# A mixture-of-experts block: expert outputs added by accumulating transfers into three DRAM sums, in place of one DRAM row for each token and choice

## The chip, the core and the metric

The kernel runs on one core of one Trainium2 chip. The metric is the device time in microseconds (us) of one execution. Three runs of the kernel before took 300.21, 301.05 and 305.1 us; their median is 301.05 us.

## What is computed

The input is x, two sequences of 512 tokens with 256 channels, so 1024 tokens. A first part (a gated recurrence over time, with layer norms) changes x. A second part is a mixture of experts, and this is where the change lies. Cut to what matters:

```python
probs = jax.nn.softmax(x @ gate_w.T, axis=-1)             # 64 experts
topk_w, topk_idx = jax.lax.top_k(probs, 6)                 # 6 experts for each token
topk_w = topk_w / jnp.sum(topk_w, axis=-1, keepdims=True)
combine = jnp.sum(one_hot(topk_idx, 64) * topk_w[..., None], axis=1)
h = silu(einsum('th,eih->tei', x, experts_w1))             # 176 hidden channels
y = einsum('tei,ehi->teh', h, experts_w2)
routed_out = einsum('teh,te->th', y, combine)
out = routed_out + shared_out                              # shared_out: one dense expert
```

Every output row is x plus the layer norm of this sum. Each token's routed output is thus the sum of six rows that six different experts produce, each with a weight.

## The kernel before, in words

**Tiles.** The 1024 tokens are 8 tiles of 128 (`NTT`). The 64 experts are taken in 32 groups of two (`G`, `NG`). An expert has room for one block of 128 tokens in the fast path; what an expert gets beyond that is handled by one further block (`further`, run once in steps between the groups as a "float"), and by a loop whose count is read at run time (`tc.For_i`, L1007). The loop's body is not entered for these inputs.

**Stages, in order of time.**

1. *Mixing* (0 to about 115 us). Channels are mixed, and for each token tile `token_tile` (L473) computes the gate, picks six experts, and finds for each choice a slot in a DRAM array `xs_d`. VectorE (DVE), ScalarE (ACT) and TensorE (PE) instructions are interleaved by the class `Turns` (L314), a small planner that emits pieces of several streams by estimated costs: each piece says `yield spent(n)`, and the planner's clock moves on by that. A removed piece therefore also shifts the places of the pieces behind it.
2. *Scatter.* Each token tile issues six indirect transfers on GpSimd (POOL) (L576) that copy the tile's rows into `xs_d`. A row of `tok` has the 256 channels, then 64 weights (`C:DEST`), then 64 destination numbers (`DEST:`), 384 words in all. The destination numbers are made by one running sum (scan) over the 64 experts on DVE (L561): the number of the row of `y_d` into which this token's output of this expert goes. `xs_d` is filled beforehand with blank rows (L173, four transfers of 3072 KB on the SyncE queue), whose destination number lies beyond the end, so that unused rows are skipped later.
3. *Experts* (about 140 to 266 us). For each group of two experts, SP loads the rows (`load`, L879, four groups ahead, five buffers `xg`); `turn` (L882) transposes them on PE and copies each row's weight and destination into `cols` (12 buffers); `up` and `turn_h` compute the hidden layer; `down` (L928) multiplies by the second matrix; ACT scales the result by the weight into `y` (L940, six buffers, each for a pair of experts); and `collect` (L863) issues an indirect transfer on POOL that writes the 128 rows of `y` to their rows of `y_d`. `y_d` has 6144 rows of 256 words, one for each token and choice. All 65 of these transfers are declared independent of each other. The weights are loaded by SP into 19 buffers, 13 of the 32 groups in buffers used before.
4. *Tail* (about 266 us to the end). Each queue waits for all the collects and passes the loop's barrier. Then 16 loads of 384 KB (L1021), half issued by SP and half by ACT, bring in six rows for each token (`yk`). `total_up` (L1025) adds three of them to the other three on DVE, and PE adds those and the shared output (`y_sh`) in PSUM; `measure` and `put_out` do the layer norm, add x, and store.

**Order of the work.** PE, DVE, ACT and SP run their instructions in the order in which the code emits them. POOL is not among those engines (`ORDERED`), so a scheduler places its instructions; it keeps the order of dependent ones. A transfer on POOL also takes one of eight completion counters in turn.

Of the kernel before, what the change touches and what calls it, by code (L numbers as in the profile page):

```python
# [18 lines left out]
P = 128  # L19
# [17 lines left out]
G = 2  # L37
NG = E // G
DEST = C + E
ROW = DEST + E  # L40
WROW = 2 * I + C
# [11 lines left out]
def block_kernel(ctx: ExitStack, tc, x, w_act, w_rec, w_val, gate, wa, wb, wb_one, sh_gu, sh_dn, out):  # L53
# [112 lines left out]
    nc.gpsimd.memset(blank[:, :DEST], 0.0)  # L166
    nc.gpsimd.iota(blank[:, DEST:].bitcast(I32), pattern=[[0, E]], base=int(FAR), channel_multiplier=0)

# [13 lines left out]


    
    first_i = const.tile([P, NTT], I32, name="first_i")
    for i in range(NTT):
        nc.gpsimd.iota(
            first_i[:, i : i + 1],
            pattern=[[0, 1]],
            base=TOPK * i * P - 1,  # L190
            channel_multiplier=TOPK,
        )
    first_f = const.tile([P, NTT], F32, name="first_f")
    nc.gpsimd.tensor_copy(first_f, first_i)
    y_d = dram.tile([NT * TOPK, C], F32, name="y_d")
    y_sh = data.tile([P, NTT, C], F32, name="y_sh")
# [148 lines left out]
    def spent(n):  # L345
        return 0.16 + n / 960
# [93 lines left out]

    hsh = carve(len(SH_CHUNKS), NT)
    tok = carve(NTT, ROW)
    sel = data.tile([P, NTT, E], BF16, name="sel")
    lg = data.tile([P, NTT, E + 10], F32, name="lg")
    nc.gpsimd.memset(lg[:, :, E : E + 2], NEG)
    none_sel = const.tile([P, E], BF16, name="none_sel")
    nc.gpsimd.memset(none_sel, 0.0)
    rank = data.tile([P, NTT, E], F32, name="rank")
# [24 lines left out]
    def token_tile(t, pv):  # L473
# [79 lines left out]
        for j in range(t):  # L553
# [5 lines left out]
        yield spent(E / 2)  # L559

        nc.vector.tensor_tensor_scan(  # L561
            tok[:, t, DEST:].bitcast(I32), sel[:, t, :], none_sel, first_f[:, t : t + 1], ALU.add, ALU.add
        )
        yield spent(2 * E)

# [190 lines left out]
    def further(now, f):  # L756
# [66 lines left out]
        nc.vector.tensor_reduce(wt, two, AX.X, ALU.add)  # L823
        nc.vector.tensor_mul(two, xg[:, DEST:].bitcast(I32), one)
        to = stat.tile([P, 1], F32, tag="to", name="to")
        nc.vector.tensor_reduce(to, two, AX.X, ALU.add)
        to_i = stat.tile([P, 1], I32, tag="to_i", name="to_i")
        nc.vector.tensor_copy(to_i, to)
        yield
# [30 lines left out]

    puts = []

    def collect(y, rows):  # L863
        ins = nc.gpsimd.indirect_dma_start(  # L864
            out=y_d[:, :],
            out_offset=bass.IndirectOffsetOnAxis(ap=rows.bitcast(U32), axis=0),
            in_=y,
            in_offset=None,
            bounds_check=TOPK * NT - 1,
            oob_is_err=False,  # L870
        ).ins

        tc.declare_no_dep(ins, group="puts", reason="rows of y_d are disjoint")
        tc.add_to_no_dep_group("puts", ins)
        puts.append(ins)

# [5 lines left out]
    def turn(xg, g):  # L882

        px = ps.tile([P, G, KC, P], F32, tag="pr", name="px", bufs=1)
        for q in range(G):
            for k in range(KC):
                nc.tensor.transpose(px[:, q, k, :], xg[:, q, ts(k, P)], ident)  # L887
        cols = hpool.tile([P, 2, G], F32, tag="cols", name="cols", bufs=12)
        flat = xg.rearrange("p q r -> p (q r)")
        for u, o in enumerate((C + g * G, DEST + g * G)):  # L890
            nc.vector.tensor_copy(cols[:, u, :].bitcast(I32), flat[:, o : o + ROW + 2 : ROW + 1].bitcast(I32))
        xT = hpool.tile([P, G, KC, P], F32, tag="xT", name="xT")
        nc.vector.tensor_copy(xT, px)  # L893
        return xT, cols
# [109 lines left out]
    count = stat.tile([P, 1], I32, tag="count", name="count")  # L1004
    nc.scalar.copy(count, total)
    left = nc.values_load(count[0:1, 0:1], min_val=0, max_val=NOV)
# [7 lines left out]
    tpool = ctx.enter_context(tc.tile_pool(name="tpool", bufs=3))  # L1014
    y_v = y_d.rearrange("(i p k) c -> p i k c", k=TOPK, p=P)
    half = TOPK // 2
    yks, pos, mvs, rstds = {}, {}, {}, {}
    for i in range(NTT):
        yks[i] = tpool.tile([P, TOPK, C], F32, tag="yk", name="yk", bufs=NTT)
        for eng, o in ((nc.sync, 0), (nc.scalar, half)):  # L1020
            ins = eng.dma_start(yks[i][:, o : o + half, :], y_v[:, i, o : o + half]).ins  # L1021
            for w in puts:
                tc.add_manual_dep(ins, w.name, SYNC, reason="reads what every block wrote")

    def total_up(i):  # L1025

        yk = yks.pop(i)
        po = pos[i] = ps.tile([P, C], F32, tag="ps", name="po")
        nc.tensor.matmul(po, ident, y_sh[:, i, :], start=True, stop=False)
        pieces = [(0, half)] if i < NTT - 2 else [(k, k + 1) for k in range(half)]  # L1030
        for o, u in pieces:
            nc.vector.tensor_add(yk[:, o:u, :], yk[:, o:u, :], yk[:, half + o : half + u, :])  # L1032
        for k in range(half):
            nc.tensor.matmul(po, ident, yk[:, k, :], start=False, stop=(k == half - 1))  # L1034

# [71 lines left out]
```

## Time and profile before

| what | value |
|---|---|
| median of three runs | 301.05 us |
| the profiled execution's own time | 299.47 us |
| its span, first to last instruction | 297.8 us |
| mean granted TensorE clock | 0.901 |
| busy: PE, DVE, ACT, POOL | 235.5, 149.0, 119.6, 124.9 us |
| HBM read, written | 46.53 MB, 33.16 MB |

How it is read: a group's row gives line, engine, operation, output and inputs, the count, busy time, mean time of one in ns, then the engine's idle time just before, and what ended most of it. A row of a timeline gives start, duration, engine, line, operation and, in brackets, the idle time before. A row of a table of stages gives the stretch, its length, each engine's busy time with the number of instructions, the granted clock, the DMA engines' mean busy share, and GB/s. In a DMA queue's row stand packets, MB, and the share of 16 engines' time; q0 is POOL's queue, q1 SP's, q10 ACT's. In names, `SPq` and `ACTq` are the queues of instructions that issue transfers.

### The profile page before, as it was taken

The numbers are of one execution on the slowest core, as the hardware profiler recorded it, in microseconds if no ns is written. First come the engines' busy times: TensorE is split into PE (matmuls) and PEld (weight loads), VectorE is DVE, ScalarE is ACT, GpSimd is POOL, SyncE is SP. The second block draws the span as 40 slices with busy tenths as digits, with TensorE's granted clock in tenths as the row PEclk, the third lists the DMA queues.
The fourth block names the chain that finished last, engine by engine and source line by source line (L and its number), as shares of the span: only waits on it lengthen the run. The fifth ranks groups of instructions, "written<-read, shape, count | busy, mean of one in ns | idle before, by whom it ended". The sixth has DMA issues, their size and how long they took to land. (4 is left out here: it accounts for less than half of the span.)

```text
span 297.8 us, 4388 instructions
## 1 busy us (share of the span) xinstructions
PE 235.5 (79%) x1258; PEld 187.0 (63%) x1258; DVE 149.0 (50%) x628; ACT 119.6 (40%) x341; POOL 124.9 (42%) x159
## 2 busy tenths in 40 slices
PE   1989833964875778966889999999999999921992
PEld 0778613853664656855767788888887787710881
DVE  3469899766759504931335423333333333201594
ACT  2494665266129428202234443333333333410241
POOL 6000006722751763780064455555555555550041
PEclk9999975885599969996999999999999999985799
DMA  7999999999662443439999999999655531116982
GB/s 239 369 402 400 391 333 351 400 391 330 263 231 100 159 161 129 167 128 345 357 343 357 350 361 359 364 357 330 203 162 157 157 111 54 60 57 206 407 306 77
DMA packets 44025, 77.58 MB, mean 261 GB/s; under 512 B 4885, under 2 KB 29578, under 8 KB 44000
## 3 DMA queue, kind: packets, MB, share of 16 engines
q1 hardware_dynamic: 36480, 58.04, 56.9%
q0 software_dynamic: 6368, 16.11, 14.7%
q10 hardware_dynamic: 1152, 3.15, 2.9%
q8 instruction: 10, 0.16, 0.2%
q14 instruction: 15, 0.12, 0.1%
HBM read 46.53 MB, written 33.16 MB: 268 GB/s over the span
## 5 line engine op out<-in xcount | busy, mean ns | idle before, releaser
L864 POOL DMA_INDIRECT y_d<-y,cols x64 | 63.1, 986 | 66.9 <-ACT y L940 55.1
L576 POOL DMA_INDIRECT xs_d<-arena,slot_i x48 | 47.7, 993 | 78.5 <-DVE m L395 40.9
L924 DVE COPY hT<-pht 128x256 f32<-128x256 f32 x32 | 13.6, 424 | 69.3 <-PE pht L922 67.7
L940 ACT ACTIVATE y<-py,cols 128x256 f32<-128x256 f32 x64 | 26.8, 470 | 29.3 <-PE py L937 27.5
L911 ACT ACTIVATE h<-ph 128x256 f32<-128x256 f32 x32 | 12.3, 384 | 48.2 <-PE ph L906 39.9
L906 PE MATMUL ph<-w_sb,xT 128*128 128x176 f32 x176 | 30.0, 313 | 0.0
L906 PEld LDWEIGHTS ph<-w_sb,xT 128*128 128x128 f32 x176 | 26.4, 190 | 0.3 <-issue 0.3
L599 PE MATMUL pgu<-x2T,sh_gu_sb 128*128 128x256 f32 (+1 forms) x96 | 25.5, 424 | 0.0
L893 DVE COPY xT<-px 128x512 f32<-128x512 f32 x32 | 21.8, 683 | 4.2 <-PE px L887 4.2
L395 DVE TENSOR_TENSOR m<-z 128x32 f32<-128x32 f32 (+7 forms) x92 | 21.9, 280 | 2.4 <-remote 1.7
L933 PE MATMUL py<-w_sb,hT 128*128 128x256 f32 x88 | 22.7, 380 | 0.0
L599 PEld LDWEIGHTS pgu<-x2T,sh_gu_sb 128*128 128x128 f32 (+1 forms) x96 | 18.9, 201 | 4.0
L458 PE MATMUL pv<-w_val_sb,z 128*128 128x256 f32 x32 | 11.4, 520 | 11.6 <-DVE z L398 10.1
L887 PE MATMUL px<-ident,xg 128*128 128x128 f32 x128 | 19.3, 273 | 0.8 <-DVE xT L893 0.8
L264 PE MATMUL pz<-xnT,arena 128*128 128x256 f32 x64 | 17.3, 434 | 1.7 <-ACT xnT L253 0.9
L264 PEld LDWEIGHTS pz<-xnT,arena 128*128 128x128 f32 x64 | 13.8, 220 | 4.9 <-ACT xnT L253 1.4
L1034 PE MATMUL po<-yk,ident 128*128 128x256 f32 x48 | 13.6, 425 | 4.0 <-DVE yk L1032 4.0
L933 PEld LDWEIGHTS py<-w_sb,hT 128*128 128x128 f32 x88 | 15.8, 190 | 1.3 <-DVE hT L924 0.2
L458 PEld LDWEIGHTS pv<-w_val_sb,z 128*128 128x128 f32 x32 | 7.9, 260 | 13.7 <-issue 9.7
L283 PE MATMUL pr<-arena,xnT 128*128 128x256 f32 x64 | 15.8, 403 | 0.0
L887 PEld LDWEIGHTS px<-ident,xg 128*128 128x128 f32 x128 | 15.0, 141 | 1.1 <-DVE xT L893 1.0
L1032 DVE TENSOR_TENSOR yk<-yk 128x768 f32<-128x768 f32 (+1 forms) x12 | 7.9, 689 | 15.3 <-DMA yk<-y_d 15.2
(203 smaller groups left out, 431.3 us busy)
## 6 DMA issues: line engine op xcount, KB each, us to landing
w_sb<-in_wa SPq DMA_DIRECT2D x22, 608.0 KB
xs_d<-blank SPq DMA_DIRECT2D x4, 3072.0 KB
xg<-xs_d SPq DMA_DIRECT2D x32, 384.0 KB
arena<-in_wa SPq DMA_DIRECT2D x10, 608.0 KB
yk<-y_d ACTq DMA_DIRECT2D x8, 384.0 KB
yk<-y_d SPq DMA_DIRECT2D x8, 384.0 KB
w_sb<-in_wb SPq DMA_DIRECT2D x22, 112.0 KB
tok_d<-arena SPq DMA_DIRECT2D x2, 768.0 KB
```

The source lines that it names most:

```text
L264: nc.tensor.matmul(pz[:, ri, :], w_act_sb[:, kk, ts(ri, P)], xnT[:, kk % KC, b, o : o + H], start=(kk == 0), stop=(kk == 3),)
L283: nc.tensor.matmul(pr[:, j, :], xnT[:, kk % KC, b, o : o + P], w_rec_sb[:, kk, :], start=(kk == 0), stop=(kk == 3),)
L395: nc.vector.tensor_mul(h, dst, low[:, u : u + 1].to_broadcast(shape))
L458: nc.tensor.matmul(pv, zs[c][:, ri, 1 + j * P : 1 + (j + 1) * P], w_val_sb[:, ri, :], start=(ri == 0), stop=(ri == 1),)
L576: ins = nc.gpsimd.indirect_dma_start(out=xs_d[:, :], out_offset=bass.IndirectOffsetOnAxis(ap=slot_i[:, t, k : k + 1].bitcast(U32), axis=0) ...
L599: nc.tensor.matmul(pgu[:n, u, :], sh_gu_sb[:, k, off : off + n], x2T[:, k, ts(c, H)], start=(k == 0), stop=(k == KC - 1),)
L864: ins = nc.gpsimd.indirect_dma_start(out=y_d[:, :], out_offset=bass.IndirectOffsetOnAxis(ap=rows.bitcast(U32), axis=0), in_=y, in_offset=None,
L887: nc.tensor.transpose(px[:, q, k, :], xg[:, q, ts(k, P)], ident)
L893: nc.vector.tensor_copy(xT, px)
L906: nc.tensor.matmul(ph[:, q, :], xT[:, q, k, :], w1[:, ts(k, I)], start=(k == 0), stop=(k == KC - 1))
L933: nc.tensor.matmul(py, hT[:, q, :], w2as[q], start=True, stop=False)
L940: nc.scalar.activation(y[:, q, :], pys[q], AF.Copy, scale=wts[q])
```

## The change

Six parts:

1. A row of `tok` and `xs_d` shrinks from 384 to 321 words: the 64 destination numbers become one, the token's own number, written once by a POOL iota. The eight scans on DVE (L561) go, with their planner costs and helper tiles.
2. `y_d` goes. Three DRAM arrays of 1024 rows (`s0_d` to `s2_d`, 1 MB each) are set to zero by three transfers on SP's queue, after the first eleven groups' weights.
3. `collect` adds instead of writing: `compute_op=ALU.add`, into the three sums in turn. The independence that was declared between collects is gone, so a collect waits until the one three back, which wrote to the same sum, has landed.
4. The weight and destination of a row are copied as before by two small DVE copies; in the further block two DVE instructions go.
5. The tail loads three rows for each token, by 24 transfers of 128 KB instead of 16 of 384 KB; DVE adds one pair, PE takes in the other row.
6. The count for the loop is copied by DVE instead of ACT.

In the instruction lists of the two kernels the engines' orders are else alike, but for small swaps of neighbours in the mixing stage (the planner's clock), and for one thing on POOL: the last of the 64 collects, which stood ahead of the loop, stands behind it. The loads of the tail on both queues wait for that collect's counter.

```diff
-ROW = DEST + E
+ROW = DEST + 1
+
+NACC = 3
...
-    nc.gpsimd.iota(blank[:, DEST:].bitcast(I32), pattern=[[0, E]], base=int(FAR), channel_multiplier=0)
+    nc.gpsimd.iota(blank[:, DEST:].bitcast(I32), pattern=[[0, 1]], base=int(FAR), channel_multiplier=0)
...
-    y_d = dram.tile([NT * TOPK, C], F32, name="y_d")
+    sums_v = []
+    for a in range(NACC):
+        s_d = dram.tile([NT, C], F32, name=f"s{a}_d")
+        sums_v.append((s_d, s_d.rearrange("(i p) c -> p i c", p=P)))
+        nc.sync.dma_start(sums_v[a][1], blank[:, :C].unsqueeze(1).to_broadcast([P, NTT, C]))
...
     tok = carve(NTT, ROW)
+    nc.gpsimd.iota(tok[:, :, DEST:].bitcast(I32), pattern=[[P, NTT], [0, 1]], base=0, channel_multiplier=1)
...
-        nc.vector.tensor_tensor_scan(
-            tok[:, t, DEST:].bitcast(I32), sel[:, t, :], none_sel, first_f[:, t : t + 1], ALU.add, ALU.add
-        )
-        yield spent(2 * E)
...
-    puts = []
+    sum_turns = cycle(range(NACC))
     def collect(y, rows):
-        ins = nc.gpsimd.indirect_dma_start(
-            out=y_d[:, :],
+        nc.gpsimd.indirect_dma_start(
+            out=sums_v[next(sum_turns)][0][:, :],
             out_offset=bass.IndirectOffsetOnAxis(ap=rows.bitcast(U32), axis=0),
             in_=y,
             in_offset=None,
-            bounds_check=TOPK * NT - 1,
+            bounds_check=NT - 1,
             oob_is_err=False,
-        ).ins
-
-        tc.declare_no_dep(ins, group="puts", reason="rows of y_d are disjoint")
-        tc.add_to_no_dep_group("puts", ins)
-        puts.append(ins)
+            compute_op=ALU.add,
+        )
...
-    nc.scalar.copy(count, total)
+    nc.vector.tensor_copy(count, total)
...
-        yks[i] = tpool.tile([P, TOPK, C], F32, tag="yk", name="yk", bufs=NTT)
-        for eng, o in ((nc.sync, 0), (nc.scalar, half)):
-            ins = eng.dma_start(yks[i][:, o : o + half, :], y_v[:, i, o : o + half]).ins
-            for w in puts:
-                tc.add_manual_dep(ins, w.name, SYNC, reason="reads what every block wrote")
+        yks[i] = tpool.tile([P, NACC, C], F32, tag="yk", name="yk", bufs=NTT)
+    for i in range(0, NTT):
+        for a in range(NACC):
+            (nc.sync, nc.scalar)[(i * NACC + a) % 2].dma_start(yks[i][:, a, :], sums_v[a][1][:, i, :])
...
-        pieces = [(0, half)] if i < NTT - 2 else [(k, k + 1) for k in range(half)]
-        for o, u in pieces:
-            nc.vector.tensor_add(yk[:, o:u, :], yk[:, o:u, :], yk[:, half + o : half + u, :])
-        for k in range(half):
-            nc.tensor.matmul(po, ident, yk[:, k, :], start=False, stop=(k == half - 1))
+        nc.tensor.matmul(po, ident, yk[:, NACC - 1, :], start=False, stop=False)
+        nc.vector.tensor_add(yk[:, 0, :], yk[:, 0, :], yk[:, 1, :])
+        nc.tensor.matmul(po, ident, yk[:, 0, :], start=False, stop=True)
```

More of the change, by code (lines that the diff above doesn't have):

```diff
@@ L180, in block_kernel @@
         load_weights(g)
[L185 to L191, printed above, removed]
-        )
-    first_f = const.tile([P, NTT], F32, name="first_f")
-    nc.gpsimd.tensor_copy(first_f, first_i)
-    y_d = dram.tile([NT * TOPK, C], F32, name="y_d")
+    sums_v = []
[3 more added lines that the diff above has]
+        nc.sync.dma_start(sums_v[a][1], blank[:, :C].unsqueeze(1).to_broadcast([P, NTT, C]))
     y_sh = data.tile([P, NTT, C], F32, name="y_sh")
@@ L445, in block_kernel @@
     nc.gpsimd.memset(lg[:, :, E : E + 2], NEG)
-    none_sel = const.tile([P, E], BF16, name="none_sel")
-    nc.gpsimd.memset(none_sel, 0.0)
     rank = data.tile([P, NTT, E], F32, name="rank")
@@ L559, in token_tile @@
         yield spent(E / 2)
-        nc.vector.tensor_tensor_scan(
-            tok[:, t, DEST:].bitcast(I32), sel[:, t, :], none_sel, first_f[:, t : t + 1], ALU.add, ALU.add
-        )
-        yield spent(2 * E)
         nc.vector.reciprocal(tsum, tsum)
@@ L823, in further @@
         nc.vector.tensor_reduce(wt, two, AX.X, ALU.add)
-        nc.vector.tensor_mul(two, xg[:, DEST:].bitcast(I32), one)
-        to = stat.tile([P, 1], F32, tag="to", name="to")
-        nc.vector.tensor_reduce(to, two, AX.X, ALU.add)
         to_i = stat.tile([P, 1], I32, tag="to_i", name="to_i")
-        nc.vector.tensor_copy(to_i, to)
+        nc.vector.tensor_copy(to_i, xg[:, DEST:].bitcast(I32))
         yield
@@ L889, in turn @@
         flat = xg.rearrange("p q r -> p (q r)")
-        for u, o in enumerate((C + g * G, DEST + g * G)):
-            nc.vector.tensor_copy(cols[:, u, :].bitcast(I32), flat[:, o : o + ROW + 2 : ROW + 1].bitcast(I32))
+        o = C + g * G
+        nc.vector.tensor_copy(cols[:, 0, :], flat[:, o : o + ROW + 2 : ROW + 1])
+        nc.vector.tensor_copy(cols[:, 1, :].bitcast(I32), xg[:, :, DEST].bitcast(I32))
         xT = hpool.tile([P, G, KC, P], F32, tag="xT", name="xT")
@@ L1014, in block_kernel @@
     tpool = ctx.enter_context(tc.tile_pool(name="tpool", bufs=3))
-    y_v = y_d.rearrange("(i p k) c -> p i k c", k=TOPK, p=P)
-    half = TOPK // 2
     yks, pos, mvs, rstds = {}, {}, {}, {}
     for i in range(NTT):
-        yks[i] = tpool.tile([P, TOPK, C], F32, tag="yk", name="yk", bufs=NTT)
-        for eng, o in ((nc.sync, 0), (nc.scalar, half)):
-            ins = eng.dma_start(yks[i][:, o : o + half, :], y_v[:, i, o : o + half]).ins
-            for w in puts:
-                tc.add_manual_dep(ins, w.name, SYNC, reason="reads what every block wrote")
+        yks[i] = tpool.tile([P, NACC, C], F32, tag="yk", name="yk", bufs=NTT)
+    for i in range(0, NTT):
+        for a in range(NACC):
+            (nc.sync, nc.scalar)[(i * NACC + a) % 2].dma_start(yks[i][:, a, :], sums_v[a][1][:, i, :])
     def total_up(i):
```

## The prediction

> **What bounds the kernel now.** I read the table of stages first, over the stretches that the order of the work suggests.
>
> ```profile
> 115.00:140.00 25.00, 20.46 (x90) 16.65 (x89) 11.13 (x48) 7.72 (x17) 14.94 (x17) 0.86 0.58 207
> 148.00:209.00 61.00, 59.23 (x375) 47.21 (x373) 23.93 (x92) 25.33 (x74) 33.24 (x34) 1.00 1.03 352
> 209.00:266.00 57.00, 53.25 (x335) 41.64 (x333) 18.89 (x69) 20.91 (x62) 30.88 (x32) 1.00 0.39 121
> 270.00:287.00 17.00, 12.43 (x43) 9.64 (x44) 8.86 (x21) 3.94 (x8) 2.04 (x3) 0.71 0.96 363
> ```
>
> The columns after the length are PE, PE's weight loads, DVE, ACT, POOL, the clock, the DMA share, GB/s. The experts' stage is bound by PE (59.23 of 61, 53.25 of 57 us). POOL is about half busy, and the DMA engines are full up to about 209 us (1.03) and then not (0.39). The tail from 270 to 287 is bound by its loads (0.96). So in the experts' stage a collect costs nothing unless POOL falls behind; in the tail bytes are time.
>
> Then the collects: the rows of groups, and the timeline.
>
> ```profile
> L864 POOL DMA_INDIRECT y_d<-y,cols x64 | 63.1, 986 | 66.9 <-ACT y L940 55.1
> L576 POOL DMA_INDIRECT xs_d<-arena,slot_i x48 | 47.7, 993 | 78.5 <-DVE m L395 40.9
> L561 DVE TENSOR_TENSOR_SCAN arena<-sel,first_f,none_sel 128x64 int32<-128x64 bf16 x8 | 2.7, 339 | 0.1
> ```
>
> ```profile
> 151.16 1.04 POOL L811 DMA_INDIRECT xg_f<-tok_d,src  x1 [0.30 <-issue]
> ...
> 157.03 0.98 POOL L864 DMA_INDIRECT y_d<-y,cols  x1 [2.22 <-ACT y L940]
> 157.67 0.22 DVE L821 TENSOR_TENSOR two<-xg_f,one 128x64 f32<-128x64 f32 x1 [4.47 <-DMA xg_f<-tok_d,src]
> ...
> 185.48 0.98 POOL L864 DMA_INDIRECT y_d<-y,cols  x1 [1.33 <-ACT y L940]
> 186.77 0.98 POOL L864 DMA_INDIRECT y_d<-y,cols  x1 [0.30 <-issue]
> 189.09 0.98 POOL L864 DMA_INDIRECT y_d<-y,cols  x1 [1.33 <-ACT y L940]
> 190.37 0.98 POOL L864 DMA_INDIRECT y_d<-y,cols  x1 [0.30 <-issue]
> ```
>
> They come in pairs, one pair each 3.61 us. With three sums, a collect and the one three back are 4.89 us apart (185.48 to 190.37), then 5.92, then 4.89: on average 5.42. That is the time a collect will have to land before POOL waits for it.
>
> How long does one take? The DMA queues in short stretches show POOL's queue moving. Between 159.5 and 161.5 us nothing of a collect moves; between 161.5 and 162.5 one does (0.09 MB); on an idle machine, from 256.75 to 257.25, the one issued at 255.29.
>
> ```profile
> q0 software_dynamic: 1, 0.00, 0.0%
> q0 software_dynamic: 48, 0.09, 27.0%
> q0 software_dynamic: 47, 0.10, 56.5%
> ```
>
> Counted in order through the irregular part of the stage, the burst at 161.5 is that of 157.03. So data starts 4.5 us after issue while the DMA engines are full, and 1.5 us after when idle (up to 2.5 in 209 to 226, beside `xg` loads). A burst lasts 0.75 us full, 0.35 idle. After it comes about 0.5 us until a waiter sees it. A plain collect thus lands in about 5.8 us under load and 2.5 to 3.5 us later.
>
> **The change part by part.**
>
> *Scans and rows.* Eight scans of 0.339 us go: 2.7 us of DVE. DVE has 9.07 of 10 us busy in 40 to 50, under 8 of 10 after; in the last tiles the scan stands directly ahead of work that PE waits for. I take half, -1.4 us; from -2.7 to +1 (the planner swaps neighbours). In the further block two DVE instructions of 0.22 us go where DVE has just waited for a gather: -0.4. Scatters stay: 48 of 0.99 us (a gather of 608-word rows takes 1.01, so width doesn't set it), and they are not what starts the experts: SP's first `xg` rows are there at 137.0, PE's warm-up ends at 140.4. The blank fill moves 10.5 MB instead of 12.6: up to -5 us of DMA time, nothing if rows of 1284 bytes are slower; the zeros add 3.1 MB, 8 us at 400 GB/s, behind the eleventh group's weights and ahead of SP's first store of `tok`, which only the gather at 151 needs. The cover is the DMA share of 0.35 to 0.6 from 80 to 130 us; without it both would cost a few us. The two `cols` copies, the pool iotas: 0, the same count and size or done in the first 5 us.
>
> *POOL's time for an accumulating collect* isn't in the trace. A gather of 48 rows takes 0.894 us, of 128 rows 1.012: 1.5 ns a row, the rest fixed. A third descriptor beside two would add about 0.1 us; twice the whole is the upper end, 2.0. I take 1.0 to 1.1; a collect with its 0.30 gap then needs 1.4 of the 1.8 us that it has.
>
> *Its landing.* Lower end: only the data takes longer. The Trainium skill (Collectives: The Full Stack, "Why ReduceScatter is half of AllGather") says that an add in the transfer needs two source reads on the same ring and halves the throughput. By that rule, 5.8 + 0.75 = 6.6 us under load, 3.3 after. The trace's row of plain collects alone (5.8) would give almost no wait. Upper end: the old row is read as late as first data comes now, 4.5 more: 10.3, and 5 later. The nearest row for such a read through POOL's queue is the gather above, issued at 151.16 and used at 157.67: 6.5 us. A read of that kind, then a write of what a plain idle collect needs behind its issue (2.5 - 1.0 = 1.5), and 0.75 for doubled data: 8.8 us under load. Later, 3.0 + 1.5: 4.5 us. I take these. A rule of the skill speaks for the wait being real: DMA: Bandwidth & Descriptors, "Rules for kernel authors", wants an accumulate on the same bytes to wait for the earlier one's semaphore, and the instruction list has that wait.
>
> *What the wait makes.* With 8.8 us, three collects take 8.8, one takes 2.96 us with the wait's own overhead, against 1.8 that come. Behind a waiting collect on POOL stand only further collects (and the gather of the further block, which is ahead of the first one that waits). They hold `y` buffers: six pairs. When a pair's buffer is wanted and the collect eleven before hasn't landed, ACT waits, and PE behind it for PSUM. I carried this through collect by collect, from the ready times of the trace: issue at the latest of ready, 1.28 us behind the last issue, and landing of the third before; 8.8 us up to 209, then 4.5. By 209 about 20 of 35 are issued; PE is held for 8.5 us in all; after that a collect takes 1.53, POOL catches up, and the last collect is 10.8 us late. With 6.6 and 3.3 the largest lag is 10.7 us, PE is never held, and at the end nothing is left. With 8.8 and 5: 17. With 10.3 and 5: 22. I take +10.
>
> *The end.*
>
> ```profile
> 265.03 0.99 POOL L864 DMA_INDIRECT y_d<-y,cols  x1 [1.97 <-ACTq L1007]
> 266.32 0.98 POOL L864 DMA_INDIRECT y_d<-y,cols  x1 [0.30 <-POOLq L1007]
> 270.11 10.31 ACTq L1021 DMA_DIRECT2D yk<-y_d  x8
> ...
> 280.45 1.28 ACT L1042 ACT_TABLE_LOAD   x1 [16.74 <-DMA yk<-y_d]
> ```
>
> Now the last collect lands 2.5 us after 266.32, the barrier takes 1.25, and the loads start at 270.1, 5.1 us behind the last but one. After the change the last stands behind the barrier: landing 4.5 + barrier 1.25 + 0.3 + landing 4.5 + 0.2 = 10.75, so the loads start 5.65 us later (3.25 with 3.3 us). Then 3.1 MB instead of 6.3 are read: at 400 GB/s 7.9 us less. But the layer norms follow. ACT is held in issuing loads; its last goes out when the 16th of 24 has landed, 8.7 us after the start (now 10.3 for the 8th of 16); the first root comes 1.7 us earlier. From there a tile takes about 1.25 us of DVE (0.36 + 0.43 + 0.18 + 0.13 + 0.16 us) instead of 1.75: four tiles, -2.0; the last tile has one add and one closing matmul instead of three: -1.4. Together -5.1. The tail is +0.5 on balance. The count on DVE (0.19 us) frees ACT of work that nothing waits for, since POOL reads it last: 0.
>
> *Sum* against the profiled execution's own 299.47 us: -1.4 - 0.4 + 10 + 0.5 = +8.7, 308.2 us. Its own time lies 1.6 under the median of 301.05, so on the runs' scale 309.8; I take 309.
>
> **The rivals.**
>
> *The wait is covered by the buffers* (34 in 100). Landing of 6.6 to 8 us under load and at most 4.5 after: POOL lags by 11 to 15 us and recovers before the end. For it: six buffers, half-empty POOL, 57 us with a DMA share of 0.39. Against it: the gather's 6.5 us. The sum is -1.4 - 0.4 + 0 to 2 - 1.9 to +0.5: 297 to 302, about 299.
>
> *Faster: the halved tail loads decide* (12). From 270 to 287 loads bound; if an accumulate lands like a plain collect when idle (2.5 us), the start is 1.65 later, and if the layer norms keep up, the loads' whole 7.9 us count: -6.2 - 1.8 - some of the scans: 291 to 293. It decides if the landing in the tail is under 3 us and PE is never held. Against it: ACT's held root and the collect behind the barrier.
>
> *POOL becomes the bound* (5). If an accumulating collect takes over 1.5 us of POOL, 1.8 with its gap is all the room; at 2.0, 64 x 2.3 = 147 us against 118: 20 to 30 late, 322. Against it: the 1.5 ns a row.
>
> **How the numbers follow.** The chain of sums holding PE has 46 in 100, at 309 (own range 303 to 317); covered 34 (295 to 302, with 3 more where small things only add); faster 12; POOL 5. 2% of 301.05 is 6 us, about what a measurement of this kernel can tell from no change. Slower: 46 + 5, of which a little stays under 307 as a little of the rest goes over: 0.51. Same: 0.37. Faster: 0.12. The range leaves out the faster case and most of POOL's: 295 to 318.
>
> **What would show it.** Right: POOL's collects waiting for a transfer instead of ACT's `y`, 2.5 to 3 us apart up to about 210, then 1.5; ACT's `y` waiting for a collect and PE's share under 9 tenths near 190 to 215; the last collect issued after the barrier. Landing: the distance of a waiting collect to the one three back. Wrong: collects still in pairs 3.61 us apart with `y` as the releaser (covered); POOL instructions of 1.5 us or more (POOL's case); first loads of the tail under 3 us later than the last but one's 5.1; and the scans, if the experts' stage doesn't start about 1.4 us earlier.

## The result and the profile after

The changed kernel takes 322.56 us, the median of four runs (321.95 to 327.63), against 303.08 us for the kernel before (300.21 to 306.78, four runs). The ratio is 1.070, with a 95% interval of 1.063 to 1.077; it compares undisturbed executions only, so it is not the quotient of these medians. The profiled execution has a span of 320.8 us, 23.0 more than before, at a mean granted clock of 0.868 (before 0.901). The experts' stage itself ran at nearly the same clock: 0.97 and 1.00 in its two stretches below, 1.00 and 1.00 before.

The two timelines give where these 23.0 us lie (rounded):

| stretch | before, us | after, us | difference |
|---|---|---|---|
| start to first collect | 148.5 | 151.5 | +3.0 |
| first collect to PE's last product for `y` | 113.6 | 115.7 | +2.1 |
| from there to the last collect but one ("POOL's tail") | 3.0 | 19.4 | +16.4 |
| from there to the start of the first load of the tail | 5.1 | 9.4 | +4.3 |
| from there to the end | 27.7 | 24.8 | -2.9 |

The rows behind the first three lines, before and after: the first collect, and PE's last product for `y`.

```profile
148.50 1.04 POOL L864 DMA_INDIRECT y_d<-y,cols  x1 [13.80 <-ACT y L940]
262.06 0.70 PE L937 MATMUL py<-arena,hT 48*128 48x256 f32 x4
...
151.50 1.66 POOL L850 DMA_INDIRECT s_d<-y,cols  x1 [13.85 <-ACT y L924]
267.22 0.70 PE L921 MATMUL py<-arena,hT 48*128 48x256 f32 x4
```

So most of the loss, 16.4 of 23.0 us, is one thing: PE is done 5 us later than before, and POOL is still issuing collects 19 us after that. The table of stages says the same; the two stretches of the experts' stage are moved by 3 us against those of the prediction, that of the tail by 26:

```profile
115.00:140.00 25.00, 20.20 (x107) 16.41 (x107) 12.31 (x58) 10.23 (x28) 15.08 (x17) 0.91 0.41 142
151.00:212.00 61.00, 58.18 (x361) 46.55 (x360) 22.12 (x85) 24.64 (x72) 38.59 (x25) 0.97 1.06 317
212.00:269.00 57.00, 55.41 (x349) 43.66 (x347) 20.40 (x75) 20.84 (x62) 46.27 (x30) 1.00 0.64 104
296.00:313.00 17.00, 11.79 (x40) 9.14 (x41) 7.54 (x28) 4.91 (x10) 2.38 (x4) 0.75 0.65 201
```

PE keeps its share (58.18 of 61, 55.41 of 57). POOL, the fifth engine column, gets through 25 instructions in the experts' first stretch where it had 34, and in their second it is busy for 46.27 of 57 us with 30 of them (30.88 with 32 before). In the tail the DMA engines are no longer full (0.65, 201 GB/s; before 0.96 and 363): half the bytes, read more slowly.

The groups of the two indirect transfers:

```profile
L850 POOL DMA_INDIRECT s_d<-y,cols x64 | 99.8, 1560 | 52.7 <-ACT y L924 21.1 <-issue 11.7 <-DMA s_d<-y,cols 9.7
L565 POOL DMA_INDIRECT xs_d<-arena,slot_i x48 | 48.1, 1003 | 81.7 <-DMA w_sb<-in_wb 45.4 <-ACT rank L563 14.8 <-issue 12.2
```

A collect that adds takes 1.56 us of POOL instead of 0.986. With the usual gap of 0.30, one collect can follow the other each 1.86 us; this is called POOL's period below. PE supplies one each 1.80 us (a pair in 3.61). The scatters are as short as they were, but the first now waits for a transfer on SP's queue.

The timeline of POOL, first under load, then later:

```profile
187.53 1.55 POOL L850 DMA_INDIRECT s_d<-y,cols  x1 [1.01 <-ACT y L924]
189.60 1.56 POOL L850 DMA_INDIRECT s_d<-y,cols  x1 [0.52 <-issue]
192.15 1.55 POOL L850 DMA_INDIRECT s_d<-y,cols  x1 [0.99 <-DMA s_d<-y,cols]
194.84 1.56 POOL L850 DMA_INDIRECT s_d<-y,cols  x1 [1.14 <-DVE cols L875]
197.37 1.55 POOL L850 DMA_INDIRECT s_d<-y,cols  x1 [0.97 <-DMA s_d<-y,cols]
199.57 1.56 POOL L850 DMA_INDIRECT s_d<-y,cols  x1 [0.65 <-DVE xT L877]
202.25 1.55 POOL L850 DMA_INDIRECT s_d<-y,cols  x1 [1.12 <-ACT y L924]
...
215.96 1.55 POOL L850 DMA_INDIRECT s_d<-y,cols  x1 [0.30 <-ACT y L924]
217.82 1.56 POOL L850 DMA_INDIRECT s_d<-y,cols  x1 [0.30 <-ACT h L895]
```

A collect and the one three back are 7.3 and 7.4 us apart (187.53, 194.84, 202.25): this is the landing under load, and a collect then takes 2.45 us. The idle time ahead of them is put down to various engines (`y`, `cols`, `xT`), which is an example of a wait for several semaphores: those had long been done, and the steady distance of three shows that it is the transfer. From 214 on the waits are nearly all gone, and then POOL's own 1.86 us sets the pace. Twenty collects after the first, POOL is 50.8 us behind it, where it was 38.3 before: 12.5 us late. At the last but one it is 18.6 later. The lag of the loaded stretch is never made up, and grows.

POOL's queue, over the stretches that follow the issue of the last collect at 292.25 (294.0 to 294.5, to 295.0, to 295.6; nothing moves from 292.1 to 294.0):

```profile
q0 software_dynamic: 14, 0.01, 57.6%
q0 software_dynamic: 49, 0.05, 75.8%
q0 software_dynamic: 80, 0.04, 52.1%
```

The burst takes about 1.4 us on an idle machine, where a plain collect's took 0.35. Over the whole execution:

```profile
q0 software_dynamic: 11824, 14.57, 23.0%
```

The queue has 11824 packets (6368 before) for fewer bytes, and 73.8 us of all 16 engines (23.0% of 320.8) instead of 43.8.

Last, the end:

```profile
286.61 1.56 POOL L850 DMA_INDIRECT s_d<-y,cols  x1 [0.38 <-issue]
292.25 1.55 POOL L850 DMA_INDIRECT s_d<-y,cols  x1 [4.08 <-issue]
295.99 1.30 SPq L1004 DMA_DIRECT2D yk<-s_d  x3
...
305.88 1.28 ACT L1021 ACT_TABLE_LOAD   x1 [34.34 <-DMA yk<-s_d]
```

The last collect stands behind the loop's barrier, 5.64 us after the one ahead of it. The loads start 3.74 us after that. ACT is held in issuing its loads for 9.9 us.

### The profile page after: what moved, and what is told of

It is laid out like the page before. It is cut to its first block, busy times and chain, and to the rows that moved or that the text cites. A ratio compares the mean times of both kernels' runs of the same rounds, so it can differ in the third digit from the quotient of the medians.

```text
span 320.8 us, 4343 instructions
## 1 busy us (share of the span) xinstructions
PE 233.6 (73%) x1242; PEld 185.1 (58%) x1242; DVE 143.1 (45%) x615; ACT 120.3 (37%) x340; POOL 161.5 (50%) x150
## 3 DMA queue, kind: packets, MB, share of 16 engines
q0 software_dynamic: 11824, 14.57, 23.0%
q10 hardware_dynamic: 1728, 1.57, 1.6%
## 5 line engine op out<-in xcount | busy, mean ns | idle before, releaser
L850 POOL DMA_INDIRECT s_d<-y,cols x64 | 99.8, 1560 | 52.7 <-ACT y L924 21.1
L890 PE MATMUL ph<-w_sb,xT 128*128 128x176 f32 x176 | 31.1, 322 | 0.0
L890 PEld LDWEIGHTS ph<-w_sb,xT 128*128 128x128 f32 x176 | 27.5, 197 | 0.3 <-issue 0.3
L588 PE MATMUL pgu<-x2T,sh_gu_sb 128*128 128x256 f32 (+1 forms) x96 | 26.4, 434 | 0.0
L1010 PE MATMUL po<-y_sh,ident 128*128 128x256 f32 x16 | 6.2, 476 | 24.0 <-issue 24.0
L917 PE MATMUL py<-w_sb,hT 128*128 128x256 f32 x88 | 22.6, 379 | 0.0
L1012 DVE TENSOR_TENSOR yk<-yk 128x256 f32<-128x256 f32 x8 | 3.3, 416 | 34.4 <-DMA yk<-s_d 34.4
L1010 PEld LDWEIGHTS po<-y_sh,ident 128*128 128x128 f32 x16 | 3.7, 242 | 25.0 <-issue 24.4
L258 PE MATMUL pz<-xnT,arena 128*128 128x256 f32 x64 | 16.0, 409 | 1.7 <-ACT xnT L247 1.0
L512 PE MATMUL pl<-gate_sb,x2T 128*128 128x64 f32 x32 | 7.7, 393 | 11.4 <-issue 8.0
L258 PEld LDWEIGHTS pz<-xnT,arena 128*128 128x128 f32 x64 | 12.9, 206 | 4.5 <-ACT xnT L247 1.4
```

What stands on the lines that cost most here:

```text
L258: nc.tensor.matmul(pz[:, ri, :], w_act_sb[:, kk, ts(ri, P)], xnT[:, kk % KC, b, o : o + H], start=(kk == 0), stop=(kk == 3),)
L588: nc.tensor.matmul(pgu[:n, u, :], sh_gu_sb[:, k, off : off + n], x2T[:, k, ts(c, H)], start=(k == 0), stop=(k == KC - 1),)
L850: nc.gpsimd.indirect_dma_start(out=sums_v[next(sum_turns)][0][:, :], out_offset=bass.IndirectOffsetOnAxis(ap=rows.bitcast(U32), axis=0), i ...
L890: nc.tensor.matmul(ph[:, q, :], xT[:, q, k, :], w1[:, ts(k, I)], start=(k == 0), stop=(k == KC - 1))
L917: nc.tensor.matmul(py, hT[:, q, :], w2as[q], start=True, stop=False)
```

## The experiments

**Theory A:** the loss takes two things together. The wait for the sum three back makes POOL lag while the DMA engines are full; and since an adding collect takes 1.86 us of POOL against a supply of 1.80, POOL never makes the lag up. Rivals: the wait alone (as predicted); POOL's time alone; the time that the adds take on the DMA engines, at PE's expense.

The runs fall into four groups, in each of which the kernel before was run again. It took 286.37 us (median) beside plain writes, eight and four sums, and adding before; 302.50 beside 384-word rows and both runs on the count; 300.54 beside two plain sums, bf16 rows and both runs with two copies; 300.45 beside the run with one copy. The first and the last group ran on the same chip at different times, so the 14 us between them aren't a property of the chip; what they are stays open. Across groups only ratios to the kernel before of the same group are compared, and stretches inside the experts' stage, where the granted clock was 0.97 to 1.00 in every profile.

**Plain writes: the wait, without adds.**

```diff
-            compute_op=ALU.add,
```

> The changed kernel with its collects writing instead of adding, so that the six outputs of a token overwrite each other in three arrays: the addition is left out, the waits on the collect three back stay. Theory A (it takes both: a wait under load that makes POOL late, and 1.86 us of POOL for each adding collect, which leaves no room to make it up): POOL's collect falls from 1.56 to 0.98 us, plain landing is 5.8 us under load, POOL lags by up to 5 us and has recovered by 266; the last collect ahead of the loop starts near 268 instead of 286.6, and the time is about 302 us. Rival B (the wait alone): the same if only the landing matters, since 5.8 us of landing in three turns are near the pace of 1.8. Rival C (something else in the new kernel, such as the row width, keeps the experts late): over 310.

Measured: 283.53 us, ratio 0.983 (0.977 to 0.989). The timeline of POOL:

```profile
182.86 0.98 POOL L850 DMA_INDIRECT s_d<-y,cols  x1 [2.88 <-DMA s_d<-y,cols]
184.24 0.98 POOL L850 DMA_INDIRECT s_d<-y,cols  x1 [0.40 <-DVE cols L874]
185.53 0.99 POOL L850 DMA_INDIRECT s_d<-y,cols  x1 [0.30 <-ACT h L894]
189.20 0.98 POOL L850 DMA_INDIRECT s_d<-y,cols  x1 [2.69 <-ACT h L894]
...
217.23 0.99 POOL L850 DMA_INDIRECT s_d<-y,cols  x1 [0.30 <-DMA s_d<-y,cols]
218.52 0.99 POOL L850 DMA_INDIRECT s_d<-y,cols  x1 [0.30 <-DMA s_d<-y,cols]
```

The wait is there (6.3 to 6.9 us from one collect to the third behind it), and POOL falls behind: twenty collects after the first it is 6.4 us late against the profile of the kernel before. But from about 205 on POOL runs at 1.29 us and has caught up by the end (115.8 us from the first to the last but one; 116.5 before). So the wait by itself costs nothing here, and the rest of the change seems to gain a little: 1.7% by the ratio, 1.0% by the medians of all executions, both under the 2% that would count as faster.

**Eight sums in turn: adds, nearly without the wait.** Three of the eight are set to zero and read back.

```diff
+NSUM = 8
...
-    for a in range(NACC):
+    for a in range(NSUM):
...
-    sum_turns = cycle(range(NACC))
+    sum_turns = cycle(range(NSUM))
```

> The changed kernel with eight sums in turn instead of three, so that a collect waits for the one eight back; only three are set to zero and only three are added in the tail, so five sums are left out of the output. Theory A: no wait is left; POOL's 1.86 us for each collect alone make the last ones about 4 us late instead of 18.6; about 308 us. Rival B (the wait alone): the collects come in pairs again and are not late; 304. Rival C (POOL's time alone makes the 18.6): no change, 322.

Measured: 292.96 us, ratio 1.022 (1.016 to 1.027). A collect takes the same 1.56 us, but the tail of POOL behind PE is gone: the last collect but one comes 4.4 us after PE's last product, where it is 19.4 with three sums. That takes the wait out of the change, and most of the loss with it. It is not all gone: from the first collect to the last but one are 123.8 us (115.8 with plain writes), 8.0 more where 3.9 was expected, and the rest lies in PE.

```profile
180.00:195.00 15.00, 13.24 (x81) 9.78 (x79) 4.82 (x16) 4.62 (x14) 12.56 (x9) 1.00 1.05 289
195.00:210.00 15.00, 13.65 (x88) 11.00 (x87) 5.83 (x20) 5.07 (x15) 10.83 (x8) 1.00 0.90 199
```

PE, the first engine column, is not full there (13.24 and 13.65 of 15), while the DMA engines have a share of 1.05 and move only 289 GB/s (the kernel before 363 between 180 and 195). In the changed kernel PE has 15.00 of 15 in both stretches.

**Four sums.** `NACC` is 4, and the tail adds two rows to the other two.

> The changed kernel with four sums, all added in the tail (two pairs on DVE, two rows on PE). Theory A: a landing of 7.4 us in four turns is 1.85, as much as POOL's own 1.86, so the wait adds almost nothing; the last collects are 4 to 6 us late; 1 MB more is read in the tail, +2.6 us; about 311 us. Rival B: 309. Rival C: 325.

Measured: 300.59 us, ratio 1.045 (1.036 to 1.053). It lies between three and eight sums, as it should if the wait grows shorter, but above the 311 us that were expected (some 1.03): four turns don't take the wait away. In the execution that was profiled, the longest of the four (303.17 us), POOL's tail is 8.3 us, also between the two.

**The kernel before with adding collects: adds, no wait at all.** `y_d` is set to zero beforehand.

```diff
     y_d = dram.tile([NT * TOPK, C], F32, name="y_d")
+    y_z = y_d.rearrange("(a i p) c -> a p i c", a=TOPK, p=P)
+    for a in range(TOPK):
+        nc.sync.dma_start(y_z[a], blank[:, :C].unsqueeze(1).to_broadcast([P, NTT, C]))
...
             oob_is_err=False,
+            compute_op=ALU.add,
```

> The kernel before with one change: its collects add into the 6144 rows of y_d, which six transfers set to zero behind the first weights. Every row is written once, so no collect waits for another. Theory A: POOL's collect takes 1.56 us, one each 1.86 against 1.805 that come: about 4 us late at the end, landing 1 us longer; +5 us, 306 to 308 us. Rival B (the wait alone): +1 us. Rival C (POOL's time alone makes the 18.6): +18 us, 320.

Measured: 300.12 us, ratio 1.045 (1.039 to 1.051), some 13 us where 5 were expected. POOL's tail is 4.4 us again, so POOL's time without the wait leaves POOL close behind PE. What was not expected is that PE itself is late: 121.8 us from the first collect to its last product. PE's waits between 180 and 210 us are led by the rows that SP loads:

```profile
PE px L891 <- DMA xg<-xs_d: 3.2, 4, 1.2
```

With adds at full pace these loads come late: the DMA engines have a share of 1.05 and move 295 GB/s between 180 and 195 us, where they moved 363 before. In the changed kernel this rival is not what costs the time, since PE is full there (15.00 of 15). (This kernel also writes 6.3 MB of zeros that the kernel before doesn't, before the first collect.)

**Rows of 384 words in the changed kernel.**

```diff
-ROW = DEST + 1
+ROW = DEST + E
```

The slices that fill and read the last words follow.

> The changed kernel with rows of 384 words again, of which the last 63 are not used. Theory: rows of 1284 bytes cost the blank fill as much time a row as those of 1536 or more, so the first scatter and the experts start late; with 384 words the first scatter starts near 46.5 instead of 50.1 and the first collect near 148.5 instead of 151.5; -3 us, about 319.5. Rival (the planner's new order or the clock of PE makes the experts late): first collect stays at 151.5, no change.

Measured: 324.85 us, ratio 1.075 (1.069 to 1.082), so no gain. But the profile shows what the narrow rows do. The stretch from 20 to 32 us, first with 321 words, then with 384:

```profile
20.00:32.00 12.00, 10.53 (x51) 8.97 (x50) 10.54 (x50) 6.90 (x11) 0.00 (x0) 1.00 1.07 306
```

```profile
20.00:32.00 12.00, 10.53 (x51) 8.97 (x50) 11.16 (x52) 6.89 (x12) 0.00 (x0) 1.00 1.06 399
```

The fill runs at 306 GB/s with rows of 1284 bytes, at 399 with 1536. A narrower row is not a quicker one: 2870 packets in these 12 us, against 3128. With 384 words the first scatter goes out at 46.54 us (46.22 before, 50.06 after), and the first collect at 147.07 (148.5 before, 151.5 after). Yet the last collect but one is at 286.56, as it was at 286.61: POOL eats the earlier start (139.5 us instead of 135.1 from the first collect to the last but one). No run shows why; with the experts 4 us earlier, more of the collects fall in the time in which the DMA engines are full, which fits theory A but is only argued.

**The count on ACT in the changed kernel, and on DVE in the kernel before.** Two kernels, the same line exchanged:

```diff
-    nc.vector.tensor_copy(count, total)
+    nc.scalar.copy(count, total)
```

> The changed kernel with the count copied by ACT again, which by the instruction list puts the last collect ahead of the loop. Theory: the last collect then follows the one before by 1.86 us and one landing and the barrier follow, so the loads of the tail start about 2.6 us earlier; about 320 us. Rival (the place of the last collect costs nothing, since its landing is hidden in the barrier): no change, 322.5.

> The kernel before with only the count copied by DVE instead of ACT, which by the instruction list puts the last collect behind the loop. Theory: two landings of 2.5 us and the barrier between them instead of one: the tail's loads start 6.75 us behind the last collect ahead of the loop instead of 5.1 behind the last but one, +1.7 us, a ratio of 1.005. Rival: no change, or a gain because the engines read the count earlier.

Measured: with the count on ACT 324.35 us, ratio 1.071 (1.065 to 1.078); the kernel before with the count on DVE 304.21 us, ratio 1.009 (1.006 to 1.011), a small loss that is clear of its interval. The end of the latter:

```profile
266.57 0.99 POOL L864 DMA_INDIRECT y_d<-y,cols  x1 [1.97 <-issue]
270.68 0.98 POOL L864 DMA_INDIRECT y_d<-y,cols  x1 [3.11 <-issue]
```

The one-instruction change of part 6 puts the last collect behind the loop: the two are 4.11 us apart instead of 1.29. It isn't the count alone that decides, though: in the changed kernel with two plain sums, and with plain writes and idle copies (both below), the count is on DVE too, and the last two collects are only 1.3 to 1.6 us apart, much as in the kernel before. Why the scheduler places the last collect in one way or the other isn't shown. In the changed kernel the count on ACT brings the loads' start from 9.4 to 6.4 us behind the last collect but one. The whole didn't become faster: in that execution the first collect came 3.1 us later than in the profiled one of the changed kernel, so this run alone leaves the price of part 6 in the changed kernel unsettled.

**Two plain sums in turn: a longer wait, without adds.**

```diff
-    sum_turns = cycle(range(NACC))
+    sum_turns = cycle(range(2))
...
-            compute_op=ALU.add,
```

> The kernel after, but with plain writes, and into two of the three sums in turn; the addition is left out and the third sum stays zero. A collect thus takes POOL's 0.98 us, and waits for the one two back. The wait by itself, made as long per collect as the prediction had it (there 8.8 us over three; here the 6.7 us between waiting collects of the run with plain writes, over two, 3.35 us). Theory (the wait holds PE if it is long enough; the recurrence of the prediction is right): under load collects 3.3 us apart, largest lag about 26 us, ACT's y waits for collects and PE is held by about 11 us, the last collect 11 to 16 us later than with three plain sums; ratio to the kernel before 1.02 to 1.04. Rival (only adds cost, by the time they take on POOL or on the DMA engines): as three plain sums, 0.98 to 0.99.

Measured: 324.25 us, ratio 1.078 (1.063 to 1.094), slower than expected. The timeline of POOL, and ACT's group for `y`:

```profile
173.63 0.98 POOL L850 DMA_INDIRECT s_d<-y,cols  x1 [4.51 <-DMA s_d<-y,cols]
174.92 0.99 POOL L850 DMA_INDIRECT s_d<-y,cols  x1 [0.30 <-issue]
180.48 0.98 POOL L850 DMA_INDIRECT s_d<-y,cols  x1 [4.57 <-DMA s_d<-y,cols]
181.77 0.99 POOL L850 DMA_INDIRECT s_d<-y,cols  x1 [0.30 <-issue]
```

```profile
L923 ACT ACTIVATE y<-py,cols 128x256 f32<-128x256 f32 x64 | 26.9, 471 | 60.0 <-DMA s_d<-y,cols 34.9 <-PE py L920 16.0 <-PE ph L889 5.6
```

A pair each 6.85 us, `y` waits 34.9 us for collects, and PE's part of the stage is 119.9 us (112.8 with three plain sums). So the wait is able to do alone what the prediction had it do, if it is long enough. The last collect but one is 22.6 us late instead of 11 to 16. The term that the expectation had too small is the landing after the load: there a collect takes 1.56 us on average, over a wait of two, so some 3.1 us, and more where both waits follow each other.

**Idle work on POOL: POOL's time without adds.** Behind each collect of the plain kernel, two small copies, and in a later run only the first:

```diff
+        for n in (C, 1):
+            nc.gpsimd.tensor_copy(junk[:, :n], y[:, :n])
```

> The kernel after with plain writes (the addition is left out), three sums in turn and the wait for the one three back kept, and with each collect two idle copies on POOL (128x256 and 128x1) that bring POOL's time for a collect to about the 1.86 us of an adding one. No adds on the DMA engines. Theory A (POOL's time and the wait together make the lag): with 6.7 us between waiting collects under load and 2.5 later, the last collect is 11 to 14 us later than with plain writes alone; ratio 1.02 to 1.03. Rival B (it is what the adds take of the DMA engines): as plain writes alone, 0.98 to 0.99.

> The kernel before with the same two idle copies on POOL behind each collect: POOL's time alone, no wait, no adds, no other bytes. Theory A: POOL is 3 to 4 us late at the end, ratio 1.01 to 1.015; the 1.045 of the kernel before with adding collects then holds some 9 us that are the transfers' own. If POOL's time were all of it: 1.045.

> As the plain writes into three sums with two idle copies, but with one copy (128x256, 0.41 us) behind each collect: POOL's period should fall between the 1.29 us of plain collects and the 2.03 of two copies, I expect 1.57 to 1.8. The addition is left out. Theory A (a lag built up by the wait under load, about 10 us here with 6.7 us between waiting collects, is made up only as far as POOL's period is below the supply of 1.80): last collect late by 2 us at a period of 1.57, 5 at 1.65, 7 at 1.70, 10 at 1.80 (12.5 at 1.86), against 0 with plain writes alone and about 19 with two copies. Rival (POOL is only in the way where its period is over the supply of 1.80): not late below 1.80.

Measured: the plain kernel (three sums, wait kept) with two copies 325.75 us, ratio 1.081 (1.068 to 1.095); the kernel before (no wait) with two copies 319.93 us, ratio 1.068 (1.057 to 1.079); the plain kernel with one copy 304.10 us, ratio 1.017 (1.011 to 1.023), over executions from 299.0 to 307.1 us. Both runs with two copies missed, because the copies came out too costly. The timeline of POOL in the kernel before with two copies:

```profile
188.34 0.98 POOL L865 DMA_INDIRECT y_d<-y,cols  x1 [0.62 <-issue]
189.32 0.42 POOL L878 COPY junk<-y 128x256 f32<-128x256 f32 x1
189.90 0.98 POOL L865 DMA_INDIRECT y_d<-y,cols  x1 [0.17 <-issue]
190.89 0.91 POOL L878 COPY junk<-y 128x1 f32<-128x1 f32 x3
192.42 0.98 POOL L865 DMA_INDIRECT y_d<-y,cols  x1 [0.62 <-issue]
```

A pair takes 4.08 us, 2.04 for a collect, not the 1.86 that was wanted: 0.24 over the supply, times 64, is 15 us, and that is what POOL's tail shows (18.8 us, 15.8 more than before). With one copy it takes 1.55:

```profile
215.64 0.98 POOL L851 DMA_INDIRECT s_d<-y,cols  x1 [0.17 <-issue]
217.20 0.98 POOL L851 DMA_INDIRECT s_d<-y,cols  x1 [0.17 <-issue]
218.75 0.98 POOL L851 DMA_INDIRECT s_d<-y,cols  x1 [0.17 <-ACT y L926]
```

Here POOL's tail is 5.4 us, 2.4 over the 3.0 of plain writes, where the expectation had 2 for a period of 1.57. So a POOL that is quicker than the supply can still end late, since it has the lag of the loaded stretch to make up. This speaks against the rival that only a period above 1.80 hurts, by 2.4 us in one profile. Put together:

| kernel | POOL's period, us | waits for | first collect to PE's last product | POOL's tail | ratio |
|---|---|---|---|---|---|
| before | 1.28 | nothing | 113.6 | 3.0 | 1 |
| three plain sums | 1.29 | third back | 112.8 | 3.0 | 0.983 |
| three plain, one copy | 1.55 | third back | 113.4 | 5.4 | 1.017 |
| **after**: three sums | 1.86 | third back | 115.7 | 19.4 | 1.070 |
| three plain, two copies | 2.04 | third back | 117.2 | 22.7 | 1.081 |
| before, two copies | 2.04 | nothing | 117.2 | 18.8 | 1.068 |
| eight sums | 1.86 | eighth back | 119.4 | 4.4 | 1.022 |
| before, adding | 1.86 | nothing | 121.8 | 4.4 | 1.045 |
| two plain sums | 1.29 | second back | 119.9 | 18.5 | 1.078 |

The ratios hold more than these two columns: between three plain sums with and without one copy they differ by 3.4%, some 10 us, of which the columns show 3. The columns come from one profiled execution each. The one with a copy took 299.01 us, the shortest of six, 0.995 of the median of the kernel before; that of plain sums took 283.34 us, 0.989. These two agree with the columns, and the 1.017 says little. Besides, the two are of different groups: in that where the kernel before takes 286 us, the first collect comes at 133 to 136 us, in the others at 147 to 155, and what the mixing stage adds to each ratio can't be told. The columns are what the comparison rests on.

Theory A stands at the period of the changed kernel: 1.86 without the wait leaves a tail of 4.4 us, the wait at 1.29 leaves 3.0, and both together 19.4. Two limits remain. PE is slower in the two kernels with adds and no wait, which shortens their tails; counted from the first collect to the last but one, the changed kernel is 18.6 us later than the kernel before and eight sums 7.3, so that the wait accounts for 11.3 us of it. And no run has a period of 1.86 without adds: with the wait, 1.55 leaves a tail of 5.4 us and 2.04 one of 22.7, so that 1.86 lies between them by argument only. At 2.04 POOL's time alone is enough, and the wait adds only 3.9.

**The kernel before with rows in bf16.** Plain writes and half the bytes in the tail, without an add in the transfer: the kernel before with `y`, `y_d` and `yk` in bf16. All six rows are added by PE.

```diff
-    y_d = dram.tile([NT * TOPK, C], F32, name="y_d")
+    y_d = dram.tile([NT * TOPK, C], BF16, name="y_d")
...
-        pieces = [(0, half)] if i < NTT - 2 else [(k, k + 1) for k in range(half)]
-        for o, u in pieces:
-            nc.vector.tensor_add(yk[:, o:u, :], yk[:, o:u, :], yk[:, half + o : half + u, :])
-        for k in range(half):
-            nc.tensor.matmul(po, ident, yk[:, k, :], start=False, stop=(k == half - 1))
+        for k in range(TOPK):
+            nc.tensor.matmul(po, ident_b, yk[:, k, :], start=False, stop=(k == TOPK - 1))
```

> The kernel before with y, y_d and the tail's rows in bf16 instead of f32 (the six rows of a token are rounded to bf16), and all six rows of a token added by PE in PSUM, none by DVE. Half the bytes in the tail without an add in a transfer, a wait or more packets. If the tail's bytes are what the change could win (as the run with plain writes says, 5 us): 292 to 296 where the kernel before takes 300, ratio 0.97 to 0.985, loads still starting 5.1 us behind the last collect but one. Rival (the tail is as long because ACT's root comes late and the layer norms follow at their own pace): ratio 0.99 to 1.00.

Measured: 294.09 us, ratio 0.985 (0.973 to 0.996): faster than both kernels, though than the kernel before by less than 2%.

```profile
266.84 0.99 POOL L866 DMA_INDIRECT y_d<-y,cols  x1 [1.97 <-ACTq L1009]
268.14 0.98 POOL L866 DMA_INDIRECT y_d<-y,cols  x1 [0.30 <-POOLq L1009]
272.10 7.41 ACTq L1023 DMA_DIRECT2D yk<-y_d  x8
...
279.54 1.28 ACT L1041 ACT_TABLE_LOAD   x1 [14.01 <-DMA yk<-y_d]
```

The loads start 5.26 us behind the last collect but one, as in the kernel before. ACT is free after 7.4 us instead of 10.3, and from the loads' start to the end are 20.6 us instead of 27.7. This gains more of the tail (7.1 us) than the three sums do (2.9), with nothing added to POOL; it rounds six rows for each token to bf16. The additions on DVE go at the same time, and how much of the 7.1 us is theirs isn't separated.

## Why the prediction was wrong

The kind of thing was right, its size and its place were not. A kernel made slower by the wait in the collects was the likeliest case, at 309 us and up to 317 in its own range; 322.6 lies outside both that and the range given.

**POOL's time for an adding collect: the step that failed.** The prediction took 1.0 to 1.1 us of POOL, from the 1.5 ns a row by which a 48-row gather is shorter than a 128-row one, and so a period of 1.4 us in 1.8. It is 1.56, with the gap 1.86. The row used was one of a transfer without an add. The upper end, twice the whole, was given as 2.0 and its 20 to 30 us as a rival of 5 in 100. That rival is half of the truth: it named "over 1.5 us" as the point, and its 322 us came out, but by luck: it belongs to a period of 2.3, and the loss isn't POOL's time alone. By the prediction's own recurrence (issue at the latest of three times), POOL at 1.86 without the wait is 3.9 us late.

**The landing.** Predicted 8.8 us under load, measured 7.4; and at the end 4.5, measured 3.7 from issue to the start of the loads. The burst was taken as 0.75 us longer; idle it grew from 0.35 to 1.4. The rule of the Trainium skill that is cited there (Collectives: The Full Stack, "Why ReduceScatter is half of AllGather"), that an add in the transfer halves the throughput, falls short of that fourfold burst, and of the packets and time of POOL's queue: 5584 packets and 41.1 us of all engines with plain writes (14.6% of 281.6), 11824 and 73.8 with adds. That is 96 packets and 0.50 us of 16 engines more for each of 65 collects.

```profile
q0 software_dynamic: 5584, 14.56, 14.6%
```

**What the wait makes.** The mechanism held: collects waiting for the third back, 2.45 us apart under load, close to the 2.5 to 3 that was said. The consequence was put in the wrong place. Predicted: PE held for 8.5 us, then POOL catching up at 1.53, the last collect 10.8 late. Found: PE's part only 2.1 us longer, `y` waiting for a collect only from 254 us on, for 1.1, 1.1 and at last 1.8 us:

```profile
266.13 0.84 ACT L924 ACTIVATE y<-py,cols 128x256 f32<-128x256 f32 x2 [1.83 <-DMA s_d<-y,cols]
```

and no catching up. Put through the same recurrence: landings of 7.4 and 3.7 with the 1.28 us of POOL that the recurrence was carried with (the period of 1.4 taken above hardly changes it) give a last collect 2.5 us late, so the prediction's own 10.8 needed the landing that it had too long; with 1.86, 18.5 late, against 18.6 measured. The 2.5 is a low end: two collects between 223 and 236 us still took 6.3 and 6.4 us to land, and with 5 us for the whole later part the recurrence leaves some 10 (an estimate from the ready times of the profile before). At 1.86 the later landing doesn't matter as long as it is under three periods, 5.6 us. So the recurrence held; two of its inputs were off, in opposite directions, and at the measured landings it is the one on POOL that makes the 18.5.

**Scans, rows, fill.** Predicted -1.4 us for the scans and nothing for the fill "if rows of 1284 bytes are slower". They are slower, and it wasn't nothing: the first scatter is 3.8 us later and waits for a transfer, the first collect 3.0 later. With rows of 384 words the first collect comes 1.4 us before that of the kernel before, as much as the scans were priced at. The cover that was named, a DMA share of 0.35 to 0.6, begins at 80 us; the fill lies ahead of it, under a share of 1.06. In single executions of kernels with narrow rows the first collect varied by some 5 us (149.2 to 154.6), so the 3.0 and the 1.4 have that uncertainty, and the match of the 1.4 may be luck.

**The end.** Loads predicted to start 5.65 us later behind the last collect but one, found 4.3 later; the barrier is as predicted, the landing 0.8 shorter. From there -5.1 was predicted, found -2.9: ACT is held 9.9 us by its issues (8.7 predicted, 10.3 before), since the 24 loads of 128 KB ran at 255 GB/s in their first 12 us and not at 400 (the 16 larger ones: 346 in theirs). On balance +1.4 instead of +0.5.

**Part 6 was priced at 0** for the copy, and the place of the last collect was counted under the end without naming its cause. In the kernel before, the count on DVE is enough to move the last collect behind the loop, and costs 0.9%; in the changed kernel its price isn't settled.

**The sum.** Predicted: -1.8, +10, +0.5. Found: +3.0, +18.5, +1.4. The two-plain-sums run shows that PE can be held in the way predicted; the rival "covered by the buffers" is what happens with plain writes; and the halved tail is worth only a part of what the rival "faster" said (1.0 to 1.7% with plain writes, in one group of runs). The four chances add up to 97, not 100, which decides nothing here.

## What to carry to other kernels

An engine that is half idle on average has room only for as long as its period stays below the supply, and a backlog is made up only at the difference between the two: before an instruction in a steady stream is made longer, put its new period beside the supply's, and take it from a row of the same kind or carry both ends to the bottom line. A wait that costs nothing alone and a longer period that costs a little can cost much together. And bytes can be taken out of a stage without giving the saved time back to an engine that feeds it, as with the narrower data type and the same transfers on POOL here, where the rounding is allowed.

## What was not expected of the hardware

An accumulating indirect transfer of 128 rows of 1 KB took 1.56 us of POOL (plain 0.98), some 96 packets and 0.50 us of 16 DMA engines more, and landed in 7.4 us under load (6.3 to 6.9 plain). With accumulates at full pace the DMA engines had a share of 1.05 at 289 and 295 GB/s, where plain traffic reached 363. Filling DRAM with rows of 1284 bytes ran at 306 GB/s, with rows of 1536 bytes at 399: no more rows in a microsecond (2870 packets in 12 us, against 3128). The tail's loads of 128 KB in rows of 1 KB ran at 255 GB/s over their first 12 us, those of 384 KB at 346.
